# Keys loaded at a pace, reciprocals two steps later, and work moved between the blocks of the feed-forward, in a sandwich of attention and ternary feed-forward

## The chip, the core and the metric

The kernel runs on one core of a Trainium2 chip. The core has five engines that run side by side: TensorE (PE), which multiplies matrices; VectorE (DVE); ScalarE (ACT), which evaluates functions such as exp; GpSimd (POOL); and SyncE (SP), which here only issues transfers (DMAs). The engines meet through semaphores, and each works through its own instructions in order. The metric is the device time of one launch in microseconds (us), median of several runs.

## The reference

One input x of 4096 tokens by 256 features passes through attention and through a feed-forward. Each is given a normalized input and its output is normalized before it is added to the stream.

```python
def _layernorm(x, axis=-1, eps=1e-05):
    m = jnp.mean(x, axis=axis, keepdims=True)
    v = jnp.var(x, axis=axis, keepdims=True)
    return (x - m) / jnp.sqrt(v + eps)

# attention: H = 16 heads of 16, causal, float32
qkv = x @ w_attn + b_attn
logits = jnp.einsum('bhqd,bhkd->bhqk', q, k) * scale
logits = jnp.where(causal[None, None, :, :], logits, -jnp.inf)
weights = jax.nn.softmax(logits, axis=-1)
out = jnp.einsum('bhqk,bhkd->bhqd', weights, v)
return out.transpose(0, 2, 1, 3).reshape(b, n, d) @ w_proj + b_proj

# feed-forward: weights of -1, 0 and 1, tlin(x, w, s) = (x @ w.T) * s
h = jax.nn.silu(tlin(x, w1_w, w1_s)) * tlin(x, w2_w, w2_s)      # 256 -> 1024
h = jax.nn.gelu(tlin(h, h1_w, h1_s), approximate=False)         # 1024 -> 1024
h = jax.nn.gelu(tlin(h, h2_w, h2_s), approximate=False)         # 1024 -> 1024
return tlin(h, w3_w, w3_s)                                      # 1024 -> 256

x = x + _layernorm(attn(_layernorm(x)))
x = x + _layernorm(ffn(_layernorm(x)))
```

## The kernel before

**Blocks and items.** The tokens are cut into 8 blocks of 512 (`NB`, `QB`), a block into 4 tiles of 128 (`NT`). The first stage is the attention. An item (j, g) is block j of queries with 4 of the 16 heads; there are 32 items, numbered n = 4j + g. An item's inner loop (L855) runs over the 4(j+1) tiles of keys, kt.

**Three streams in an item.** Scores (`ScoreUnit`, tile `s`) of item n are made by PE and exponentiated by ACT (`e`, L661). Two steps later PE multiplies them with the values (`Values`, tile `av`); column 16 of each head's values is 1, so a row of `av` holds the sums of the exponentials. Meanwhile the row maxima of item n+1 are found: PE makes products (`pm`, L563) and DVE reduces them (`mx`, L576). All of it is issued in an order written out by hand, for PE in turns: products for maxima, scores, products for maxima, values. PE has three banks of memory for `pm`; if DVE stops, PE stops soon after.

**Keys.** A chunk is the keys of one block for one item: two loads of 256 KB from DRAM, where each number is held as a rounded half and the rest (`halves_of`). There are 16 places (`RING`). `ask(n, kt)` (L471), called at each step, asks for chunks of up to item n+2 as soon as the place's last user has been issued. All these loads go through SP's queue, as do the loads of queries and x and the stores of results. An instruction that waits on SP holds up what stands behind it.

**Background.** A `Background` holds a queue of generators, first in, first out. `pace` (L57) does as many steps of them per kt as their planned sizes ask for (`PREP`, `PROJECT`, `NORM` = 26, 28, 12). `prep(j)` makes queries, keys and values of a block, through the transposed input `xT` (tag `T`). `project(j)` (L212) is queued when the last `av` of block j has been stored to DRAM, that is in step 0 of block j+1: it loads x again and the sums of the exponentials (L221, tile `sums`), lets 3 steps pass, takes the reciprocals on DVE (L224), stores them, loads the attention's output (`o`) and the reciprocals spread over the heads (`inv`), multiplies them on POOL, projects on PE (`py`), normalizes and stores the stream as `x1[j]`. `norm_block(j)` (L290) loads `x1[j]`, normalizes it on DVE with a power on POOL (L172), and transposes it on PE (`ptf`); a function then takes the transposed features.

**Into the feed-forward.** In the last two items of attention `norm_block(0)` runs too; `first_features` (L771) lets ACT copy the result to `xT0` in float32. After the attention POOL issues loads of the scales (L892, L901), and a flag in memory decides between two branches; the profile took the first (`halves`), which holds for weights that survive the rounding. There the weights stay in memory, and each activation is a rounded half and the rest, on which PE multiplies one after the other. New pools of memory take over the places that the attention's pools held; the first use of such a pool waits for all users of what was there.

**A block of the feed-forward** (L1007): 8 output chunks with `za` = w1 and `zb` = w2 (L1011), Silu on ACT, a product `fa` on DVE (L1016) and the halving on DVE (`settle`, L965 and L966); then 8 chunks each of h1 and h2 (`z`, L1027) with Gelu and the halving; then 4 tiles of w3 (`pyf`, L1042), scaled, normalized, added to `x1` and stored (L1049 to L1058). Beside it runs a Background of its own, one step per output chunk: in block 0 first `project(7)`, queued ahead of the loop, then `norm_block(1)`, with two steps per chunk in h1 and h2; in the others `norm_block(j + 1)`.

Of the kernel before, what the change touches and what calls it, by code (L numbers as in the profile page):

```python
# [10 lines left out]
F32 = mybir.dt.float32  # L11
F32R = mybir.dt.float32r
AF = mybir.ActivationFunctionType
ALU = mybir.AluOpType
# [3 lines left out]
P = 128  # L18
QB = 512
NT = QB // P  # L20
# [47 lines left out]
def sandwich_kernel(  # L68
# [19 lines left out]
    nc = tc.nc  # L88
# [79 lines left out]
    def layernorm_rstd(mv):  # L168
        ve = stat.tile([P, NT], F32, tag="ve", name="ve")
        nc.vector.tensor_scalar_add(ve, mv[:, :, 1], EPS)  # L170
        rstd = stat.tile([P, NT], F32, tag="rstd", name="rstd")
        nc.gpsimd.tensor_tensor(rstd, ve, neghalf, ALU.pow)  # L172
        return rstd
# [38 lines left out]
    def project(j, room):  # L212
# [9 lines left out]
        for _ in range(3):  # L222
            yield True
# [96 lines left out]


    xT0 = const.tile([P, DC, QB], F32, tag="xT0", name="xT0")


    with ExitStack() as actx:
# [16 lines left out]
        class Room:  # L342
# [5 lines left out]
            def features(self, j):  # L348
                return [wk1.tile([P, DC, QB], F32, tag=t, name=f"{t}_{j}") for t in ("o", "inv")]
# [540 lines left out]
    def load_scale(pool, src, tag):  # L890
        s = pool.tile([P, FC], F32, tag=tag, name=tag)
        nc.gpsimd.dma_start(out=s, in_=src.rearrange("(c p) -> p c", p=P))  # L892
        return s

    fs = ctx.enter_context(tc.tile_pool(name="fs", bufs=1))
    s1 = load_scale(fs, w1_s, "s1")
    s2 = load_scale(fs, w2_s, "s2")
    sh1 = load_scale(fs, h1_s, "sh1")
    sh2 = load_scale(fs, h2_s, "sh2")
    s3 = fs.tile([P, D], F32, tag="s3", name="s3")  # L900
    nc.gpsimd.dma_start(out=s3, in_=w3_s.partition_broadcast(P))  # L901

    def feed_forward(halves):
# [6 lines left out]
        with ExitStack() as fctx:  # L910
# [23 lines left out]

            w3_r = fw.tile([P, FC, D], F32R, tag="w3", name=f"w3_{parts}")
            w3_sb = w3_r.bitcast(F32)
            if halves:
                tiles = {**W, "h2": weight_pieces("h2", TAGS["h2"])}
                load_pieces(rounded["h2"], tiles["h2"])
# [64 lines left out]
            room, bg = Room(), Background()  # L1004
            keep_features(0)([xT0[:, c, :] for c in range(DC)])
            bg.add("project", project(NB - 1, room), PROJECT)
            for j in range(NB):  # L1007
                xT = xTs[j]
                ha = activations(FC, f"ha{parts}_{j}")
                for oc in range(FC):  # L1010
# [9 lines left out]
                    bg.step()  # L1020
                if j + 1 < NB:
                    bg.add("norm", norm_block(j + 1, room, keep_features(j + 1)), NORM)
                src = ha
                for layer, (key, sc) in enumerate((("h1", sh1), ("h2", sh2))):
                    hb = activations(FC, f"hb{parts}_{j}_{layer}")
                    for oc in range(FC):
# [5 lines left out]
                        if j == 0:  # L1032
                            bg.step()
# [17 lines left out]
                rstd = layernorm_rstd(mv)  # L1051
                for t in range(NT):
                    normalize(y[:, t, :], y[:, t, :], mv, rstd, t)
                    nc.gpsimd.tensor_tensor(y[:, t, :], y[:, t, :], xb[j][:, t, :], ALU.add)  # L1054
                nc.sync.dma_start(
                    out=out[j * QB : (j + 1) * QB, :].rearrange("(t p) d -> p t d", p=P),
                    in_=y,
                )  # L1058
# [41 lines left out]
```

## Time and profile before

| | |
|---|---|
| median of 3 runs | 2531.14 us (2525.56 to 2536.95) |
| the profiled execution | 2537.64 us, its span 2535.9 us |
| mean granted clock of TensorE | 0.973 |
| busy: PE, DVE, ACT, POOL | 2415.0, 1787.8, 1310.2, 561.0 us |
| attention; feed-forward | to about 1813 us; from there on |
| DMA | 202.73 MB, mean 80 GB/s |

The span is that from the first to the last instruction; around it lie 1.7 us. A row of the profile names the engine, the line of the kernel, the operation and the tiles (out<-in). In brackets behind an instruction stands the idle time of its engine before it, and what ended it. `SPq` is SP issuing a transfer. Rows of a table of stretches give, behind the stretch, its length, the busy time (with the number of instructions) of PE, of PE's weight loads, of DVE, ACT and POOL, then PE's granted clock as a share of full speed, the share of the DMA engines that was busy, and GB/s.

### The profile page before, as it was taken

What the parts mean: (1) busy time and instruction counts of PE and PEld (TensorE: products, weight loads), DVE (VectorE), ACT (ScalarE), POOL (GpSimd) and SP (SyncE); (2) the same over time, 40 slices, a digit from 0 to 9 for tenths busy, and PEclk for the clock granted to TensorE, in tenths of its full rate; (3) what the DMA queues carried; (4) which work ended last, traced back from release to release, by engine and by line L of the source; (5) the groups of instructions that cost most, each with busy time, mean ns of one, the idle gap of its engine ahead of it and who ended that gap; (6) DMA issues with size and microseconds to landing.
All of it is one profiled execution on the core that took longest, in us unless ns stands there. A gap on an engine that the chain in (4) does not pass through costs nothing. (4 is left out here: it accounts for less than half of the span.)

```text
span 2535.9 us, 40119 instructions
## 1 busy us (share of the span) xinstructions
PE 2415.0 (95%) x15237; PEld 1437.1 (57%) x15237; DVE 1787.8 (70%) x3834; ACT 1310.2 (52%) x1712; POOL 561.0 (22%) x896
## 2 busy tenths in 40 slices
PE   5889999999999999999999999999899999999998
PEld 2545444545454454454555555544478787787776
DVE  1667887888897888797999989984145535554553
ACT  1336665666675667675766667767612222222221
POOL 2325332423243233322422231000120000000000
PEclk8779999999999999999999999999989999999999
DMA  4434434324233322423222232111310000000000
GB/s 154 158 127 153 133 115 161 96 98 130 98 126 126 101 71 72 158 92 130 92 77 66 88 100 73 51 43 51 100 34 17 17 1 17 17 17 1 17 9 10
DMA packets 134777, 202.73 MB, mean 80 GB/s; under 512 B 14864, under 2 KB 59536, under 8 KB 134576
## 3 DMA queue, kind: packets, MB, share of 16 engines
q1 hardware_dynamic: 132624, 198.75, 23.6%
q8 instruction: 122, 2.00, 0.3%
q10 hardware_dynamic: 1776, 1.18, 0.2%
q0 software_dynamic: 176, 0.15, 0.1%
q14 instruction: 79, 0.65, 0.1%
HBM read 137.91 MB, written 62.13 MB: 79 GB/s over the span
## 5 line engine op out<-in xcount | busy, mean ns | idle before, releaser
L661 ACT ACTIVATE e<-s 128x1024 f32<-128x1024 f32 (+3 forms) x1175 | 1038.7, 936 | 487.0 <-PE s L646 481.4
L576 DVE TENSOR_REDUCE mx<-pm 128x1 f32<-128x512 f32 x1792 | 1111.8, 682 | 161.0 <-PE pm L563 144.6
L563 PE MATMUL pm<-k,q 64*128 64x512 f32 (+3 forms) x2304 | 627.2, 455 | 44.8 <-DVE mx L576 33.0
L563 PEld LDWEIGHTS pm<-k,q 64*128 64x128 f32 x2304 | 324.1, 188 | 546.5 <-DVE mx L576 384.8
L696 PE MATMUL av<-e,v 128*32 128x512 f32 (+3 forms) x4608 | 584.4, 579 | 1.5 <-POOL e L666 1.5
L646 PE MATMUL s<-q,k 64*128 64x512 f32 (+3 forms) x2304 | 471.7, 391 | 4.4 <-ACT xT L515 1.3
L646 PE MATMUL s<-mrow,ones 64*128 64x512 f32 (+3 forms) x2304 | 458.1, 381 | 0.0
L1029 ACT ACTIVATE fb<-z,sh 128x512 f32<-128x512 f32 x128 | 88.1, 688 | 400.0 <-PE z L995 381.2
L580 DVE CUSTOM_DVE_ANT_0 pm<-pm,mask 128x384 f32<-128x384 f32 (+3 forms) x512 | 240.0, 517 | 76.5 <-PE pm L563 72.2
L646 PEld LDWEIGHTS s<-q,k 64*128 64x128 f32 x2304 | 235.8, 189 | 72.3 <-issue 18.4
L646 PEld LDWEIGHTS s<-mrow,ones 64*128 64x128 f32 x2304 | 240.7, 188 | 38.1 <-DVE mrow L620 0.7
L666 POOL TENSOR_SCALAR_AFFINE_SELECT e<-e 128x256 f32<-128x256 f32 x256 | 102.5, 407 | 637.4 <-ACT e L661 635.5
L995 PE MATMUL z<-hb_0h,h 128*128 128x512 f32 x512 | 203.8, 398 | 0.0
L995 PE MATMUL z<-hb_0l,h 128*128 128x512 f32 x512 | 203.0, 396 | 0.0
L696 PEld LDWEIGHTS av<-e,v 128*32 128x32 f32 x4608 | 91.8, 108 | 145.1 <-issue 129.9
L172 POOL TENSOR_TENSOR rstd<-ve,neghalf 128x4 f32<-128x4 f32 x19 | 19.3, 1015 | 687.3 <-DVE ve L170 661.6
L965 DVE CAST hb_1h<-fb 128x512 fp32r<-128x512 f32 x64 | 27.4, 428 | 150.7 <-ACT fb L1029 150.7
L965 DVE CAST hb_0h<-fb 128x512 fp32r<-128x512 f32 x64 | 28.3, 442 | 141.3 <-ACT fb L1029 141.3
L1014 ACT ACTIVATE sl<-za,s 128x512 f32<-128x512 f32 x64 | 44.1, 689 | 130.9 <-DVE fa L1016 65.7
L995 PEld LDWEIGHTS z<-hb_0l,h 128*128 128x128 f32 x512 | 97.1, 190 | 22.6
L995 PEld LDWEIGHTS z<-hb_0h,h 128*128 128x128 f32 x512 | 97.1, 190 | 22.6
L748 POOL CAST wh<-wc 128x256 fp32r<-128x256 f32 x88 | 34.9, 397 | 232.2 <-DMA wc<-in_h_t_dram 185.1
(247 smaller groups left out, 2463.9 us busy)
## 6 DMA issues: line engine op xcount, KB each, us to landing
k<-k SPq DMA_DIRECT2D x288, 256.0 KB
q<-q SPq DMA_DIRECT2D x64, 256.0 KB
x<-in_x_dram SPq DMA_DIRECT2D x16, 512.0 KB
k<-hik SPq DMA_DIRECT2D x32, 256.0 KB
k<-lok SPq DMA_DIRECT2D x32, 256.0 KB
q<-hiq SPq DMA_DIRECT2D x32, 256.0 KB
q<-loq SPq DMA_DIRECT2D x32, 256.0 KB
avd<-av_sb SPq DMA_DIRECT2D x32, 256.0 KB
```

The lines of the kernel that those rows point to most:

```text
L563: nc.tensor.matmul(ps[:, 0:n], lhsT=qT[j, g][pr][r, t * P : (t + 1) * P], rhs=kT[G * j + g, c, pr][r, 0:n], start=True, stop=True,)
L576: nc.vector.tensor_reduce(self.mx[:, h, c : c + 1], ps[:, 0:n], AX.X, ALU.max)
L580: nc.vector.tensor_tensor_reduce(out=ps[:, 0:n], in0=ps[:, 0:n], in1=mask[:, QB - n : QB], scale=1.0, scalar=-3.0e38, op0=ALU.add, op1=ALU ...
L646: nc.tensor.matmul(self.ps[i][:, self.q0 :], lhsT=(self.k, ones[pr])[m][r, :], rhs=(qT[j, g][pr], mT[j, g])[m][r, self.q0 :], start=(m == ...
L661: nc.scalar.activation(e[:, at : at + n, q0:], ps[:, :, q0:], AF.Exp)
L666: nc.gpsimd.affine_select(out=at, in_=at, compare_op=ALU.is_ge, fill=0.0, base=0, pattern=[[0, 2], [1, P]], channel_multiplier=-1,)
L696: nc.tensor.matmul(self.av[h * HW : (h + 1) * HW, q0:], lhsT=vb[kt // NT][:, kt % NT, o : o + HW], rhs=es[h // 2][:, h % 2, q0:], start=(k ...
L748: nc.gpsimd.tensor_copy(hi, w)
L965: nc.vector.tensor_copy(hi, full)
L995: nc.tensor.matmul(ps, lhsT=w[c], rhs=single(part[:, c, :]), start=(c == 0 and i == 0), stop=(c == kc - 1 and i == parts - 1),)
L1014: nc.scalar.activation(sl, za, AF.Silu, scale=s1[:, oc : oc + 1])
L1029: nc.scalar.activation(h, z, AF.Gelu, scale=sc[:, oc : oc + 1])
```

## The change

1. `ask`: from item 8 on (block 2), keys are asked for only at even kt, one chunk at a time.
2. `project`: 5 steps instead of 3 between the load of `sums` and its reciprocals, for blocks 2 to 6.
3. `first_features`: ACT writes the rounded half of `xT0`, DVE the rest; block 0 of the feed-forward reads these, without a conversion of its own.
4. The four loads of scales stand before the attention, in tiles of the constants' pool; `s3` is loaded inside the branch.
5. `project(7)` is queued in block 1 of the feed-forward, behind its w1 and w2, and the two steps per chunk are block 1's.
6. In the last block of the feed-forward each tile has its own power, normalization, sum and store, one tile behind the products; the sum of the last tile is DVE's.
7. Memory: `inv` shares the place of `xT` (tag `T`); the features of the feed-forward have one buffer (pool `f1`) instead of two.

```diff
     def layernorm_rstd(mv):
+        n = mv.shape[1]
...
-        nc.gpsimd.tensor_tensor(rstd, ve, neghalf, ALU.pow)
+        nc.gpsimd.tensor_tensor(rstd, ve, neghalf[:, 0:n], ALU.pow)
...
-        for _ in range(3):
+        for _ in range(5 if 1 < j < NB - 1 else 3):
             yield True
         nc.vector.reciprocal(sums, sums)
...
+    def load_scale(pool, src, tag):
+        s = pool.tile([P, FC], F32, tag=tag, name=tag)
+        nc.gpsimd.dma_start(out=s, in_=src.rearrange("(c p) -> p c", p=P))
+        return s
+
+    s1 = load_scale(const, w1_s, "s1")
+    s2 = load_scale(const, w2_s, "s2")
+    sh1 = load_scale(const, h1_s, "sh1")
+    sh2 = load_scale(const, h2_s, "sh2")
-    xT0 = const.tile([P, DC, QB], F32, tag="xT0", name="xT0")
+    xT0 = [
+        const.tile([P, DC, QB], F32R, tag=f"xT0{p}", name=f"xT0{p}") for p in "hl"
+    ]
...
-                return [wk1.tile([P, DC, QB], F32, tag=t, name=f"{t}_{j}") for t in ("o", "inv")]
+                return [wk1.tile([P, DC, QB], F32, tag=t, name=f"{t}o_{j}") for t in ("o", "T")]
...
                 if asked[0] >= RING and chunks[asked[0] - RING] >= (n, (kt - 1) // NT):
                     return
+                if n >= 2 * G and kt % 2:
+                    return
                 keys(*chunks[asked[0]])
+                if n >= 2 * G:
+                    return
...
-                nc.scalar.copy(xT0[:, c, :], pts[c])
+                hi, lo = (t[:, c, :] for t in xT0)
+                nc.scalar.copy(hi, pts[c])
+                nc.vector.tensor_tensor(lo, pts[c], hi, ALU.subtract)
...
+            s3 = fw.tile([P, D], F32, tag="s3", name=f"s3_{parts}")
+            nc.gpsimd.dma_start(out=s3, in_=w3_s.partition_broadcast(P))
...
-                    hp.tile([P, n, QB], F32, tag=f"h{n}{p}", name=f"{name}{p}")
+                    (f1 if halves and n == DC else hp).tile(
+                        [P, n, QB], F32, tag=f"h{n}{p}", name=f"{name}{p}"
+                    )
...
-            keep_features(0)([xT0[:, c, :] for c in range(DC)])
-            bg.add("project", project(NB - 1, room), PROJECT)
+            xTs[0] = [t.bitcast(F32) for t in xT0]
+            due = []
+
+            def leave(j, y, mv, ts, rstd):
+                for i, t in enumerate(range(ts.start, ts.stop)):
+                    nc.vector.tensor_scalar(
+                        y[:, t, :], y[:, t, :], mv[:, t, 0:1], rstd[:, i : i + 1],
+                        ALU.subtract, ALU.mult,
+                    )
+                    (nc.vector if (j, t) == (NB - 1, NT - 1) else nc.gpsimd).tensor_tensor(
+                        y[:, t, :], y[:, t, :], xb[j][:, t, :], ALU.add
+                    )
+                nc.sync.dma_start(
+                    out=out[j * QB + ts.start * P : j * QB + ts.stop * P, :].rearrange(
+                        "(t p) d -> p t d", p=P
+                    ),
+                    in_=y[:, ts, :],
+                )
...
+                if j == 1:
+                    bg.add("project", project(NB - 1, room), PROJECT)
...
-                        if j == 0:
+                        if j == 1:
                             bg.step()
...
+                    if j == NB - 1:
+                        one = slice(t, t + 1)
+                        due.append((j, y, mv, one, layernorm_rstd(mv[:, one, :])))
+                        while len(due) > (t < NT - 1):
+                            leave(*due.pop(0))
+                if j < NB - 1:
+                    leave(j, y, mv, slice(0, NT), layernorm_rstd(mv))
```

More of the change, by code (lines that the diff above doesn't have):

```diff
@@ L168, in layernorm_rstd @@
     def layernorm_rstd(mv):
-        ve = stat.tile([P, NT], F32, tag="ve", name="ve")
+        n = mv.shape[1]
+        ve = stat.tile([P, n], F32, tag=f"ve{n}", name="ve")
         nc.vector.tensor_scalar_add(ve, mv[:, :, 1], EPS)
-        rstd = stat.tile([P, NT], F32, tag="rstd", name="rstd")
-        nc.gpsimd.tensor_tensor(rstd, ve, neghalf, ALU.pow)
+        rstd = stat.tile([P, n], F32, tag=f"rstd{n}", name="rstd")
+        nc.gpsimd.tensor_tensor(rstd, ve, neghalf[:, 0:n], ALU.pow)
         return rstd
@@ L887, in sandwich_kernel @@
         bg.finish()
[L890 to L901, printed above, removed]
     def feed_forward(halves):
@@ L933, in tokens @@
                     return f1.tile([P, NT, D], F32, tag="y", name=f"yn_{j}_{parts}")
+            s3 = fw.tile([P, D], F32, tag="s3", name=f"s3_{parts}")
+            nc.gpsimd.dma_start(out=s3, in_=w3_s.partition_broadcast(P))
             w3_r = fw.tile([P, FC, D], F32R, tag="w3", name=f"w3_{parts}")
             w3_sb = w3_r.bitcast(F32)
+            room, bg = Room(), Background()
             if halves:
@@ L1002, in linear @@
                 return ps
-            room, bg = Room(), Background()
-            keep_features(0)([xT0[:, c, :] for c in range(DC)])
-            bg.add("project", project(NB - 1, room), PROJECT)
+            xTs[0] = [t.bitcast(F32) for t in xT0]
+            if not halves:
+                xTs[0] = activations(DC, "xTf0")
+                nc.vector.tensor_tensor(xTs[0][0], *xT0, ALU.add)
+            due = []
[14 more added lines that the diff above has]
+                )
             for j in range(NB):
@@ L1050, in feed_forward @@
                     layernorm_stats(y[:, t, :], mv, t)
[L1051 to L1058, printed above, removed]
+                    if j == NB - 1:
[5 more added lines that the diff above has]
+                    leave(j, y, mv, slice(0, NT), layernorm_rstd(mv))
     low = nc.values_load(flag, min_val=0, max_val=1)
```

## The prediction

> **What bounds the kernel now.** I read the page first: TensorE (PE) is busy 2415.0 of 2535.9 us, so what can be won is in the 121 us where it is not, and in the time when its clock is halved.
>
> ```profile
> span 2535.9 us, 40119 instructions
> PE 2415.0 (95%) x15237; PEld 1437.1 (57%) x15237; DVE 1787.8 (70%) x3834; ACT 1310.2 (52%) x1712; POOL 561.0 (22%) x896
> ```
>
> The view of waits then shows who could be late for PE at a place that the change touches: `sums` makes VectorE (DVE) wait seven times (us in total, times, longest), and SP's issue of that load waits for the store of `avd` to land.
>
> ```profile
> DVE sums L224 <- DMA sums<-avd: 23.9, 7, 7.0
> ...
> SPq L221 <- DMA avd<-av_sb: 24.0, 7, 4.8
> ```
>
> The times of those waits, from the instructions in order of time, give the places. A table of 20 us stretches from the beginnings of blocks 2 to 7 gives the price: busy PE in the third column, its clock in the column of 1.00s.
>
> ```profile
> 272.00:292.00 20.00, 17.11 (x113) 7.82 (x110) 13.53 (x35) 11.04 (x12) 2.97 (x4) 0.83 0.56 174
> 434.00:454.00 20.00, 16.66 (x106) 7.92 (x104) 12.67 (x28) 10.03 (x11) 4.66 (x6) 0.83 0.49 165
> 636.00:656.00 20.00, 17.52 (x132) 9.13 (x132) 15.79 (x33) 12.13 (x14) 7.64 (x10) 1.00 0.52 176
> 878.00:898.00 20.00, 18.38 (x128) 9.05 (x124) 15.51 (x32) 12.08 (x13) 8.00 (x10) 0.91 0.61 185
> 1163.00:1183.00 20.00, 16.15 (x100) 7.16 (x99) 11.60 (x26) 9.53 (x10) 5.93 (x8) 0.83 0.63 208
> 1478.00:1498.00 20.00, 20.00 (x152) 10.70 (x151) 18.13 (x38) 15.13 (x17) 4.04 (x6) 1.00 0.54 164
> ```
>
> Idle PE is 2.9, 3.3, 2.5, 1.6, 3.9 and 0 us; lost clock, (1 - clock) x 20, is 3.4, 3.4, 0, 1.8, 3.4 and 0. In between PE is full (296.3 of 300 us from 1200 to 1500), so neither is made good later. Block 7 shows what an undisturbed start looks like, and SP's order of issue says why:
>
> ```profile
> 868.84 3.82 SPq L443 DMA_DIRECT2D k<-k  x8
> 873.37 0.32 SPq L707 DMA_DIRECT2D avd<-av_sb  x1
> 879.15 0.58 SPq L221 DMA_DIRECT2D sums<-avd  x1
> ...
> 1479.27 0.32 SPq L707 DMA_DIRECT2D avd<-av_sb  x1
> 1481.52 0.55 SPq L221 DMA_DIRECT2D sums<-avd  x1
> ```
>
> With eight key loads (2 MB) ahead of it, the store of `avd` lands 5.8 us after issue; with none, 2.25 us.
>
> **Part 1: keys paced, reciprocals later.** At the start of an item 6, 8, 10, 8 and 4 key loads (blocks 2 to 6) become 2. The store should land some 2.2 to 3 us after issue, not 4.9 to 5.8; `sums` then lands 2.2 us later (277.04 to 279.27), 2 to 3 us earlier than now. The two added yields move the reciprocal by one step of the key loop in block 3 (the pace there, 52 / 46, gives two background steps each) and by two in blocks 4 to 7 (52 / 58 and less give one), at 2.7 us a step (1479.78, 1482.48 and 1485.18 for the `av` products). Waits of 3.2, 3.5, 2.7, 1.8 and 4.4 us lose 2 to 8 us each: only block 2, which gets the pacing alone, may keep some 0.3 us. Gain: idle 2.9 + 3.3 + 2.5 + 1.6 + 3.9 = 14.2, clock 3.4 + 3.4 + 0 + 1.8 + 3.4 = 12.0, together 26.2, less 0.3 = **25.9**.
>
> Here a rule weighs against me. The Trainium skill (TensorE: Matmul & The Clock Gate, section "What's actually happening") lets the clock fall after an idle window of about 3.4 us. By it only block 6's gap of 3.9 us costs clock, and part 1 would give 14.2 + 3.4 - 0.3 = 17.3. The rows show halved clock after gaps of 1.6, 2.9 and 3.3 us, none after 2.5. I take the rows; the difference of 8.6 goes into the range.
>
> What else moves: `project` yields 29 times against a planned size of 28, so its store of `x1` falls out of the pace; in block 6, with no `prep` behind it, it waits for block 7. Its reader is far off in the feed-forward: nothing. `inv` now shares `T` with `xT`; both belong to one first-in-first-out background, each done before the other begins: nothing, and without that cover one `inv` landing, about 4.9 us of POOL's wait, off PE's path. Later keys: block 7 loads chunk c of item n+2 at step 4c+6 instead of 4c+5. Its last chunk still comes at step 0 of item n+1 and is first needed about step 4: 10 us of slack.
>
> **Part 2: from attention to feed-forward.**
>
> ```profile
> 1811.42 1.14 POOL L892 DMA_DIRECT2D s<-in_w_s_dram  x1 [0.20 <-issue]
> 1813.06 0.41 PE L696 MATMUL av<-e,v 128*32 128x128 f32 x4 [1.38 <-POOL e L666]
> 1816.86 1.14 ACT L980 CAST xTf_0h<-xT 128x512 fp32r<-128x512 f32 x2 [2.76 <-DMA avd<-av_sb]
> 1821.72 0.75 DVE L1016 SCALAR_TENSOR_TENSOR fa<-zb,s,sl 128x512 f32<-128x512 f32 x1 [2.92 <-issue]
> 1836.62 0.55 DVE L224 RECIPROCAL sums<-sums 128x64 f32<-128x64 f32 x1 [7.00 <-DMA sums<-avd]
> 1845.49 0.51 PE L995 MATMUL z<-ha_0l,h 128*128 128x512 f32 x1 [1.18 <-DVE ha_0l L966]
> ```
>
> Four things in a row go: the scale load that POOL runs ahead of the last mask (1.38 us of PE), the conversion, which waits for the last store's landing, the wait for `s2` (DVE stands until 1821.72), and the reciprocal's 7.0 us, behind which four `fa` are queued. New path: last `av` 1813.06 - 1.38 = 1811.68, end 1812.1; copy of `av` 0.6, and `za` starts near 1812.8, as its inputs stand in tiles that attention never gave up. Silu needs its table (1.28) and `za`: 1814.2 to 1814.9. DVE takes eight rounds of 1.86 (1823.94 to 1825.81): 1814.9 + 14.9 = 1829.8, where now it is 1845.4. Gain 15.6, and the halved window that I read behind it (8 products of 0.63 from 1846.4) 1.7: **17.3**. If Silu's tile too waits for the store (landing 1815.4, then table 1.28 and Silu 0.7), DVE starts at 1817.4 and the gain is 14.8: the low end. PE's eight rounds of 1.87 stay under DVE's.
>
> Moved to block 1: SP's loads of x, `sums`, o and inv twice each and stores of `invd` and `x1`; POOL's two products and norm; 16 `py` products of 3.5 us. They cost there what they cost here, and SP issues them behind the store of block 0's result, no longer behind 16 loads of h2. The load of `s3` (0.56 us of POOL) is wanted only by block 0's last products, 70 us on: nothing. `sums` can land during w1 and w2, at least 15 us before its reciprocal in h1: no wait. The double steps keep one flaw: norm and transposes are background steps 27 and 28. Now they share one output chunk in block 0, and PE stands 3.74 us at 1884.5; with 2k+1 and 2k+2 as a chunk's steps they share chunk 13 in block 1. Zero gain. The single-buffered features are written only after the block's w1 and w2 products: nothing.
>
> **Part 3: the end.** Now: `ve` 2525.47, power 1.02, four normalizations, four sums on POOL (to 2530.23), store at 2530.26, landed 2533.45. After: the same to 2526.78, one normalization 0.55 and one sum on DVE 0.42, store at about 2527.9 behind that of tile 2. Gain 2.4, and some 1.0 because 128 KB land sooner than 512 KB (not shown; 0 to 1.5, the time in which 512 KB passed): **3.4**. The extra DVE work per earlier tile (0.17 + 0.55) fits the 1.9 us that PE needs for a tile.
>
> **Part 4: costs.** Four scale loads stand at the start, 3.8 us of POOL (1.14, 0.91, 2 x 0.88), which is not wanted before 14.28. Their packets are another matter: from 2 to 9 us the DMA engines are full (share 1.02), and the products wait for `wp` until 9.35. In the trace one load is 16 packets of about 0.35 us, one an engine: 4 x 0.35 = 1.4 at worst, 0 if they fall behind `wp`; I take **1.2**. First features: DVE gets two subtractions (0.69 each) that wait for ACT's casts, with the maxima, and so PE's `pm`, behind them, and both score buffers stay held: 0 to 1.6, I take **0.8**.
>
> **Sum.** 25.9 + 17.3 + 3.4 - 1.2 - 0.8 = 44.6. The profiled execution took 2537.6 (span and 1.7 around it): 2493.0. It lies 6.5 over the median of the runs, 2531.1; if the same waits were in those, 2486.5. Some of the 6.5 may be waits that go anyway: I take **2490**.
>
> **Rivals.** (a) Attention recovers only idle time, or half its waits stay because `sums` is late for another reason: -9 to -15, about 2502. For it: the rule above; against it, block 7. (b) Small waits of PE for DVE fall too, as bursts of keys thin out: up to 10 more, 2480. (c) Most gains go to new waits in the same places (DVE behind `sums` again, feed-forward bound by the store): 2525. Against it: all the named waits have a shown releaser that moves. (d) Slower: keys late. In blocks 5 to 7 the ring is the limit; if loads landed over 10 us later than now, PE would stop in each item. It takes 12.7 + 41 = 54 us over 12 items, 4.5 us each, thus keys about 15 us late, to end at 2544. Only one wait of PE for a key load, 2.4 us near 80, stands in the profile.
>
> **How the numbers follow.** Likeliest 0.72 (2482 to 2499), (a) 0.12, (b) 0.08, (c) 0.05, (d) 0.03. The range from 2478 to 2506 leaves out (c), (d) and the far parts of (a) and (b). Within 0.5% (12.7 us, about what a measurement tells from no change) is most of (c): faster 0.93, same 0.04, slower 0.03.
>
> **What would show it.** Right: `sums` holds DVE under 1 us in blocks 2 to 7; the clock is 1.00 in the rows above; `za` begins within 1 us of the last `av`; the reciprocal of block 7 waits for nothing; a gap near 3.7 us before the transposes in block 1; start later by about 1 us. Wrong: PE waiting for `k`, `za` waiting for the store, or as many halved windows as now.

## The result, and the profile after

The kernel after takes 2493.03 us (median of 6 runs, 2490.62 to 2495.86), the kernel before beside it 2534.47 us: a ratio of 0.984 (95% interval 0.9825 to 0.9858), or 41 us. The forecast was 2490 with a range from 2478 to 2506. The profiled execution took 2495.86 us. Its page begins:

```profile
span 2494.2 us, 40139 instructions
PE 2395.7 (96%) x15237; PEld 1434.2 (58%) x15237; DVE 1786.7 (72%) x3838; ACT 1309.1 (52%) x1710; POOL 561.6 (23%) x898
```

The same 15237 products keep PE busy 19.3 us less than before, although no product was taken out. Part of that is clock; the rest, as will be seen, is that one kind of product became faster.

The view of waits (us in total, times, longest) answers the two rows on `sums`: VectorE waits 2.8 us instead of 23.9.

```profile
DVE sums L225 <- DMA sums<-avd: 2.8, 2, 2.6
```

Of these 2.8, block 1 has 2.6, where neither half of part 1 is at work, and block 2 has 0.26 (0.17 to 1.72 in the other eight traces of kernels with both halves). These are the 20 us stretches at the beginnings of blocks 2 to 7, with the columns as before (third column PE busy, the column of 1.00s its clock):

```profile
276.00:296.00 20.00, 20.00 (x136) 10.26 (x133) 17.34 (x45) 12.22 (x13) 6.50 (x7) 1.00 0.49 154
434.00:454.00 20.00, 19.60 (x137) 10.11 (x135) 17.17 (x40) 12.22 (x13) 6.40 (x7) 1.00 0.52 162
636.00:656.00 20.00, 20.00 (x156) 10.50 (x156) 18.46 (x42) 14.40 (x15) 6.17 (x8) 1.00 0.43 132
873.00:893.00 20.00, 20.00 (x153) 10.23 (x154) 18.47 (x37) 14.57 (x16) 6.12 (x8) 1.00 0.51 156
1155.00:1175.00 20.00, 20.00 (x154) 10.29 (x154) 18.45 (x37) 14.49 (x15) 7.99 (x10) 1.00 0.67 206
1475.00:1495.00 20.00, 20.00 (x156) 10.37 (x155) 18.35 (x37) 14.26 (x15) 5.81 (x7) 1.00 0.44 134
```

PE is full and at full clock in all but 0.4 us. SP's order of issue at block 5 shows why: two key loads stand ahead of the store, not eight, and the load of the sums, which waits for the store, follows 2.3 us later instead of 5.8.

```profile
858.54 0.90 SPq L456 DMA_DIRECT2D k<-k  x2
863.06 0.32 SPq L725 DMA_DIRECT2D avd<-av_sb  x1
863.43 0.43 SPq L113 DMA_DIRECT2D x<-in_x_dram  x1
865.36 0.59 SPq L222 DMA_DIRECT2D sums<-avd  x1
```

From attention to feed-forward (instructions in order of time; in brackets the idle time before one, and what ended it). First the row of before, then those of after:

```profile
1817.53 0.79 PE L995 MATMUL za<-xTf_0h,w 128*128 128x512 f32 x1 [4.06 <-ACT xTf_0h L980]
```

```profile
1797.36 0.58 ACT L723 COPY av_sb<-av 128x512 f32<-128x512 f32 x1 [1.13 <-PE av L714]
1798.00 0.50 PE L1007 MATMUL za<-xT0h,w 128*128 128x512 f32 x1 [0.69 <-ACT av_sb L723]
...
1799.27 1.28 ACT L1046 ACT_TABLE_LOAD   x1 [1.33 <-PE za L1007]
...
1801.29 0.75 DVE L1048 SCALAR_TENSOR_TENSOR fa<-zb,s,sl 128x512 f32<-128x512 f32 x1 [72.24 <-ACT sl L1046]
```

`za` starts 0.69 us after the last `av`, where it stood 4.06 us before, and VectorE starts 0.7 us after Silu's table is there. Silu's tile did not wait for the store: what ACT stands for, 1.33 us ahead of its table, is `za`. The table follows `za` instead of running beside it, and VectorE starts 4.0 us after the end of the last `av`, some 1.2 us later than the forecast had it.

What got worse is at the start; the gap ahead of the transposes has moved to block 1. First the two rows of before, then those of after:

```profile
9.35 2.05 PE L811 MATMUL pb<-wp,bv 128*128 128x256 f32 x4 [9.35 <-DMA wp<-in_w_proj_dram]
...
1888.21 2.21 PE L307 MATMUL ptf<-ident,yn 128*128 128x128 f32 x8 [3.74 <-DVE yn L176]
```

```profile
3.75 1.76 POOL L324 DMA_DIRECT2D sh<-in_h_s_dram  x2
...
12.10 2.05 PE L831 MATMUL pb<-wp,bv 128*128 128x256 f32 x4 [12.10 <-DMA wp<-in_w_proj_dram]
...
1956.11 2.21 PE L308 MATMUL ptf<-ident,yn 128*128 128x128 f32 x8 [3.74 <-DVE yn L177]
```

The first product starts at 12.10 instead of 9.35; the gap of 3.74 us ahead of the transposes stands in block 1 now.

By stages of the two profiled executions (us; the ends of a stage are starts of PE's products or of the copy of the last `av`; the last product counts to its end):

| stage | before | after | gain | forecast |
|---|---|---|---|---|
| to the first product | 9.35 | 12.10 | -2.75 | -1.2 |
| first product to copy of the last `av` | 1804.2 | 1785.3 | 18.9 | 25.9 - 0.8 |
| from there to block 2 of the feed-forward | 195.0 | 177.7 | 17.3 | 17.3 |
| block 2 to the last product | 515.8 | 510.9 | 4.9 | 0 |
| last product to the end | 11.6 | 8.2 | 3.4 | 3.4 |
| sum | 2535.9 | 2494.2 | 41.8 | 44.6 |

The sum is near, but it hides two errors of opposite sign: attention gave 6 us less than forecast in this pair of profiles, and blocks that the forecast held unchanged became faster. The experiments begin with the second.

### The profile page after: what moved, and what is told of

It is laid out like the page before. It is cut to its first block, busy times and chain, and to the rows that moved or that the text cites. A ratio compares the mean times of both kernels' runs of the same rounds, so it can differ in the third digit from the quotient of the medians.

```text
span 2494.2 us, 40139 instructions
## 1 busy us (share of the span) xinstructions
PE 2395.7 (96%) x15237; PEld 1434.2 (58%) x15237; DVE 1786.7 (72%) x3838; ACT 1309.1 (52%) x1710; POOL 561.6 (23%) x898
## 4 chain that ended last, share of the span: by engine, by line
PE 82%; DVE 11%; issue 2%; DMA 2%; ACT 1%; POOL 1%; SPq 0%; ACTq 0%; POOLq 0%; DVEq 0%
PE av L714 20%; PE s L664 18%; PE z L1007 18%; PE pm L581 16%; DVE mx L594 3%; DVE pm L598 2%; PE pyf L1076 2%; DVE fa L1048 2%; PE pk L426 1%; PE py L249 1%; PE pv L543 1%; PE pq L426 1%; PE pmt L630 1%; PE za L1007 1%; PE zb L1007 1%
## 5 line engine op out<-in xcount | busy, mean ns | idle before, releaser
L173 POOL TENSOR_TENSOR rstd<-ve,neghalf 128x4 f32<-128x4 f32 (+1 forms) x22 | 20.7, 943 | 662.9 <-DVE ve L171 637.4
L977 DVE CAST hb_0h<-fb 128x512 fp32r<-128x512 f32 x64 | 27.3, 427 | 138.7 <-ACT fb L1063 138.7
L1048 DVE SCALAR_TENSOR_TENSOR fa<-zb,s,sl 128x512 f32<-128x512 f32 x64 | 47.6, 745 | 72.2 <-ACT sl L1046 72.2
```

The costliest lines, as they stand in the source:

```text
L977: nc.vector.tensor_copy(hi, full)
L1048: nc.vector.scalar_tensor_tensor(h, zb, s2[:, oc : oc + 1], sl, ALU.mult, ALU.mult)
```

## The experiments

Times beside a run are medians. Each is set against the kernel before, run beside it on the same chip (2532 to 2534 us in the three sets of runs), and against the kernel after (2493.0; once more in the last set: 2491.7).

### 1 and 2. Why feed-forward blocks became faster

A block of the steady feed-forward takes 86.15 us before and 84.90 after, with the same products. From the starts of the products in the trace, those of `z` follow each other at a median of 232 ns before and 227 after (their pitch), while `py` (216), `pyf` (120) and a full item of the attention (75.4 us) are unchanged. What differs is the place of the tiles in memory (addresses are those of the built kernels; a trace does not hold them). The change moved sizes about, and the feed-forward's own tiles, the activations among them, start 128 bytes past a multiple of 256 before and at a multiple of 256 after; the weights of `za`, `zb` and `z` start at multiples of 256 in both. In these products the activations are the moving operand (`rhs`) and the weights the stationary one (`lhsT`). Two kernels shift the feed-forward's tiles and leave these weights where they are.

The kernel after, shifted:

```diff
+            pad = fw.tile([P, 32], F32, tag="pad", name=f"pad_{parts}")
+            nc.vector.memset(pad, 0.0)
             s3 = fw.tile([P, D], F32, tag="s3", name=f"s3_{parts}")
```

> The kernel after, with 128 bytes of unused space ahead of the feed-forward's tiles: its activations (the moving operands of za, zb, z) then start at 128 past a multiple of 256 bytes, as they did in the kernel before, and the weights stay where they are. Theory A, the start address of the moving operand sets the pace of the products: the start-to-start pitch of the z products goes from 227 back to 232 ns, a steady feed-forward block from 84.9 to 86.1 us, and the whole to about 2503 us (2500 to 2506), 10 us over the kernel after; the attention stays the same. Rival B, the blocks got faster through what moved out of block 0 or through the loads that no longer lie beside them: pitch 227, block 84.9, total within 2 us of the kernel after (2493).

The kernel before, aligned:

```diff
-        s = pool.tile([P, FC], F32, tag=tag, name=tag)
+        i = ("s1", "s2", "sh1", "sh2").index(tag) * FC
+        s = scales[:, i : i + FC]
...
+    scales = const.tile([P, D], F32, tag="junk", name="scales")
     s1 = load_scale(fs, w1_s, "s1")
```

> The kernel before, with its four scale tiles put into a dead tile of the attention, so that everything behind them lies 128 bytes lower and the activations of the feed-forward start at multiples of 256 bytes; nothing else differs. Theory A (start address of the moving operand): pitch of the z products 227 instead of 232 ns, steady block 84.9 instead of 86.1 us, total about 10 us under the kernel before (2521 to 2527 where that takes 2534). Rival B (what moved in the change made the blocks faster): pitch 232, total within 2 us of the kernel before.

The shifted one took 2503.4 us (2492.1 to 2504.5; ratio to before 0.988, 0.9864 to 0.990), the aligned one 2522.1 (2515.0 to 2531.9; 0.996, 0.9950 to 0.9972). The group of the largest `z` products in the kernels before, before aligned, after, and after shifted (busy us, mean ns of one product):

```profile
L995 PE MATMUL z<-hb_0h,h 128*128 128x512 f32 x512 | 203.8, 398 | 0.0
```

```profile
L997 PE MATMUL z<-hb_0h,h 128*128 128x512 f32 x512 | 201.0, 393 | 0.0
```

```profile
L1007 PE MATMUL z<-hb_0h,h 128*128 128x512 f32 x512 | 200.8, 392 | 0.0
```

```profile
L1009 PE MATMUL z<-hb_0h,h 128*128 128x512 f32 x512 | 204.3, 399 | 0.0
```

In these four kernels a product is 5 to 7 ns shorter where the moving operand starts at a multiple of 256. The pitch is 232, 227, 227 and 232 ns, the steady block 86.15, 84.9, 84.9 and 86.2 us. Theory A holds against its rival in both directions: the change is worth some 10 us here that it didn't set out to win. That it is the activations, and no other tile that was shifted with them, block 0 of the kernel after shows: there only the features lie elsewhere, 32 past a multiple, and `za` and `zb` have 233 to 234 ns, `z` 227. What about their address counts is the next question.

### 3. How fine the alignment is

```diff
+            if halves:
+                nc.vector.memset(fw.tile([P, 16], F32, tag="pad", name="pad64"), 0.0)
             s3 = fw.tile([P, D], F32, tag="s3", name=f"s3_{parts}")
...
                 y = f1.tile([P, NT, D], F32, tag="yf", name=f"yf{parts}_{j}")
+                if halves and j == 0:
+                    nc.gpsimd.memset(f1.tile([P, 8], F32, tag="pad", name="pad32"), 0.0)
```

> The kernel after with the feed-forward's transposed inputs (moving operand of za and zb) moved to 64 past a multiple of 256 bytes, and its hidden layers (moving operand of z) to 96 past one. Theory A, only multiples of 256 bytes give the short pitch: za, zb and z all at 231 to 234 ns. Theory B, multiples of 64 bytes are enough: za and zb 227 from block 1 on, z 232. The earlier kernels had only 32, 128 and 160 past a multiple beside 0. Time about 2503 (2498 to 2507) in A, about 2501 in B; the pitch decides, not the time.

It took 2502.8 us in its one run. `z` at 96 past a multiple has the long pitch, 232. `za` and `zb` at 64 past one have 229.5 (block 1) and 229 (block 2), between the two. Neither theory is right: here 64 costs half of what 32, 96, 128 or 160 past a multiple cost. The tiles at 32 past one are block 0's features in the kernel after, those at 160 the same tiles in the kernel of experiment 8 (235).

A trace taken for another question says that the moving operand's own address is not what counts. The kernel of experiment 10 has some small tiles fewer, and all that lies behind them, the weights too, starts 64 past a multiple of 256. Its `z` products have 227 ns, and so have `za` and `zb` from block 1 on:

```profile
L1007 PE MATMUL z<-hb_0h,h 128*128 128x512 f32 x512 | 200.3, 391 | 0.0
```

What fits all 14 traces is how far apart a product's two operands start, modulo 256 bytes: 227 ns at 0, 229 to 230 at 64, 231 to 237 at 32, 96, 128, 160 and 224 (block 0 of experiment 10, features at 32 against weights at 64: 232 to 233). `pyf` agrees where both its operands moved together, from 128 past to 0: it kept 120 ns. But with 32 between them, in the kernel of this experiment, it had 117, so in these products of 256 columns the distance costs nothing. No kernel here moved the weights alone, and why the distance counts is open.

### 4. The same for attention's scores

The queries, exponentials, values and score offsets of the attention start 96 bytes past a multiple of 256.

```diff
-        bv = aw.tile([P, DC], F32, tag="bv", name="bv")
+        first = wk1.tile([P, NT, D], F32, tag="y", name="first")
+        bv = first[:, 0, 0:DC]
...
-        bqk = aw.tile([P, 2 * DC], F32, tag="bqk", name="bqk")
+        bqk = biases
...
-        two = aw.tile([P, 2], F32, tag="two", name="two")
+        two = first[:, 1, 0:2]
...
-    neghalf = const.tile([P, NT], F32, tag="neghalf", name="neghalf")
+    small = const.tile([P, NT + 2 * DC], F32, tag="small", name="small")
+    neghalf, biases = small[:, 0:NT], small[:, NT:]
```

> The kernel after with 96 bytes of small tiles of the attention put elsewhere, so that the tiles behind them (values, score offsets, queries, exponentials) start at multiples of 256 bytes instead of 96 past one. Theory A, what held for the feed-forward's moving operands holds for the scores' too: a pair of score products takes 227 to 228 instead of 231 to 234 ns from start to start, 2304 pairs save 8 to 12 us, a full attention item is 1 to 1.5% shorter, and the total is -10 us (-6 to -18) against the kernel after. Rival B: with half-height operands the start address does not matter, or another engine paces the items: pairs as before, total within 2 us.

A miss: 2493.5 us (2491.6 to 2495.2), and the group of score products is as it was, 407 ns in the kernel after (first row) and here (second).

```profile
L664 PE MATMUL s<-q,k 64*128 64x512 f32 x1920 | 411.9, 407 | 2.0 <-ACT xT L533 1.2 <-ACT e L679 0.5
```

```profile
L666 PE MATMUL s<-q,k 64*128 64x512 f32 x1920 | 412.6, 407 | 2.0 <-ACT xT L535 1.2 <-ACT e L681 0.5
```

The commonest times for a pair of score products are 231 and 236 ns, not 227. These products run two at a time on half the rows; their keys start at multiples of 256, so the distance of the operands went from 96 to 0 here, and why it costs nothing stays open. Full height is not the condition either: the products of `pq`, 128 rows by 512 columns in plain float32, had theirs go from 96 to 0 too and take 607 ns in both kernels. The finding is shown for the feed-forward's `za`, `zb` and `z`, on rounded halves, and no further.

### 5 to 7. Pacing, delay, and both: what part 1 is made of

The kernel after with the delay undone:

```diff
-        for _ in range(5 if 1 < j < NB - 1 else 3):
+        for _ in range(3):
             yield True
```

> The kernel after with three steps instead of five between the load of the sums and the reciprocal, the pacing of the keys kept. Theory A, both halves of the first part are needed: the sums land some 4 us after the last item's store, the reciprocal reaches VectorE about 2 us too early in blocks 2 to 5 and 7 of the order (projections 1 to 6), waits 1 to 3 us each, and TensorE runs dry at those places; the waits of VectorE on the sums come to 6 to 12 us over the five projections, total +5 us (2 to 9) over the kernel after. Rival B, the pacing alone brought the gain and the delay is slack: waits under 1 us each, total within 1.5 us.

The kernel after with the pacing undone:

```diff
-                if n >= 2 * G and kt % 2:
-                    return
                 keys(*chunks[asked[0]])
-                if n >= 2 * G:
-                    return
```

> The kernel after with the keys asked for as in the kernel before (all that fit, at every step) and the five steps kept. Theory A, the pacing is what lets the store and the sums through: the store of the item's values lands 4.9 to 5.8 us after its issue instead of 2.2 at the starts of the blocks, VectorE waits 1 to 4 us on the sums in block 2 and shorter in later ones, total +9 us (5 to 15) over the kernel after. Rival B, the delay alone brought the gain: the store is late again but VectorE's wait on the sums stays under 0.5 us in every block, total within 2 us.

The kernel before with the pacing alone:

```diff
+                if n >= 2 * G and kt % 2:
+                    return
                 keys(*chunks[asked[0]])
+                if n >= 2 * G:
+                    return
```

> The kernel before with the pacing of the keys alone (from block 2 on at every second step, one chunk at a time); three steps before every reciprocal, as before. Theory A, the pacing by itself brings the first part's gain, the two further steps add nothing: the store of the values lands about 2.2 us after its issue at the starts of blocks 2 to 5, VectorE's waits on the sums of projections 1 to 6 fall from 15.6 us to under 4, and the total is 20 us (16 to 26) under the kernel before. Rival B, the two measures stand in for each other only in part, and each alone brings half: total 10 to 14 us under.

VectorE's waits on the sums at the starts of blocks 2 to 6, in us, with the time from the issue of the store to that of the load of the sums:

| kernel | time | 2 | 3 | 4 | 5 | 6 | store to load |
|---|---|---|---|---|---|---|---|
| before | 2534 | 3.21 | 3.52 | 2.67 | 1.80 | 4.43 | 4.9 to 5.8 |
| pacing alone | 2515.1 | 1.10 | 0 | 0 | 0 | 2.76 | 2.2; block 6: 5.7 |
| after without pacing | 2499.6 | 3.31 | 1.24 | 0 | 0 | 0 | 5.2 to 6.1 |
| after without delay | 2494.1 | 0.41 | 0 | 0 | 0 | 3.25 | 2.1 to 2.3; block 6: 6.0 |
| after | 2493.0 | 0.26 | 0 | 0 | 0 | 0 | 2.2 to 2.3; block 6: 5.9 |

Each half covers most of what the other covers. The pacing is what makes the store quick, and alone it brings 19 us (ratio 0.9926, 0.9902 to 0.9950), near the 20 of theory A. It leaves 1.10 us in block 2, where the delay isn't at work, and 2.76 in block 6, where 8 loads of w1 and w2 stand in the queue and the store is late whatever the keys do. There, and only there, the delay is needed. The row at block 6's beginning with the pacing alone has what its absence costs, 2.2 us of idle PE and 3.4 of clock:

```profile
1141.00:1161.00 20.00, 17.81 (x110) 8.24 (x110) 14.41 (x24) 10.66 (x12) 8.00 (x10) 0.83 0.57 175
```

The kernel after without the delay has this wait too, 3.25 us, and still no time to show for it (2491.5 to 2500.6; ratio to before 0.986, 0.9841 to 0.9875): by the median rival B is right, by the trace theory A in one of five places, and the difference is smaller than the spread of the runs. Without the pacing the store is late again everywhere, and the delay hides that in blocks 4 to 6, in part in block 3 and not at all in block 2, where it isn't at work:

```profile
277.00:297.00 20.00, 17.01 (x110) 8.02 (x103) 13.40 (x30) 10.65 (x12) 5.25 (x6) 0.83 0.39 127
437.00:457.00 20.00, 18.89 (x138) 9.79 (x130) 16.16 (x39) 12.35 (x13) 5.26 (x6) 1.00 0.44 140
637.00:657.00 20.00, 20.00 (x153) 10.10 (x154) 18.35 (x37) 14.81 (x16) 6.72 (x10) 1.00 0.40 132
```

It costs 6.5 us (ratio to before 0.988, 0.9869 to 0.9898), in the range of theory A (5 to 15).

### 8. The two costs of the change, taken out

```diff
-    s1 = load_scale(const, w1_s, "s1")
-    s2 = load_scale(const, w2_s, "s2")
-    sh1 = load_scale(const, h1_s, "sh1")
-    sh2 = load_scale(const, h2_s, "sh2")
...
+            if (j, g) == (3, 1):
+                s1, s2, sh1, sh2 = (
+                    load_scale(const, *pair)
+                    for pair in ((w1_s, "s1"), (w2_s, "s2"), (h1_s, "sh1"), (h2_s, "sh2"))
+                )
...
-                        if j == 1:
+                        if j == 1 and (layer, oc) != (0, 0):
                             bg.step()
```

> The kernel after with two edits far apart in time: the four scale loads are issued in block 3 of the attention instead of at the start, and the first double step in the feed-forward's block 1 is a single one, so that the normalisation and the transposes of the next block's tile stand on both sides of a chunk of products. Theory A: the first product starts at 9.4 us instead of 12.1 (the small scattered loads were what made the load of wp late), TensorE's gap of 3.7 us ahead of ptf falls to under 1 and the half clock behind it goes: together -8 us (-5 to -10) against the kernel after. Rival B: wp is late for another reason (first product still at 12), or the transposes then wait just as long for POOL's rstd (gap still over 2 us): the one or the other part stays, -3 to -5.

2482.6 us (2478.5 to 2485.9; ratio to before 0.979, 0.9758 to 0.9818), 10 under the kernel after. Both rows are as theory A has them:

```profile
9.41 2.05 PE L827 MATMUL pb<-wp,bv 128*128 128x256 f32 x4 [9.41 <-DMA wp<-in_w_proj_dram]
...
1951.80 1.64 PE L308 MATMUL ptf<-ident,yn 128*128 128x128 f32 x8 [0.80 <-DVE yn L177]
```

The four small loads had cost 2.7 us. The 3.74 us ahead of the transposes were the two background steps sharing a chunk, as the forecast read it: one step omitted sets a chunk of products between them, and the gap is 0.80.

### 9. Block 7's projection back in block 0

```diff
+            bg.add("project", project(NB - 1, room), PROJECT)
             due = []
...
-                if j == 1:
-                    bg.add("project", project(NB - 1, room), PROJECT)
...
-                        if j == 1:
+                        if j == 0:
                             bg.step()
```

> The kernel after with block 7's projection and its double steps put back into the feed-forward's block 0. Theory A, the move is what removes the stall after the attention: the load of the sums waits behind the weights' transfers for the last store (12 to 15 us from store to load in the kernels with it in block 0), VectorE waits 4 to 7 us on the sums, TensorE runs dry, the double steps' gap of 3.7 us goes back from block 1 to block 0, and the total is +8 us (5 to 13) over the kernel after. Rival B, without the scale loads and with the first features as halves there is enough slack in block 0: the wait on the sums is under 2 us and the total within 2 us of the kernel after.

2504.9 us (2503.0 to 2506.1; ratio to before 0.988, 0.9851 to 0.9906), 12 over the kernel after. The reciprocal waits as it did before, and PE behind it:

```profile
1808.70 1.24 SPq L222 DMA_DIRECT2D sums<-avd  x1
1816.31 0.55 DVE L225 RECIPROCAL sums<-sums 128x64 f32<-128x64 f32 x1 [7.72 <-DMA sums<-avd]
...
1817.49 0.80 PE L1007 MATMUL z<-ha_0h,h 128*128 128x512 f32 x1 [6.03 <-DVE fa L1049]
```

The load of the sums is issued 12.5 us after the store, against 14.8 in the kernel before: what else the change did there leaves the store almost as late. Theory A.

### 10. The last norm over all tiles at once

```diff
-                    if j == NB - 1:
+                    if j == NB:
...
-                if j < NB - 1:
+                if j < NB:
                     leave(j, y, mv, slice(0, NT), layernorm_rstd(mv))
```

> The kernel after with the last block's norm over all four tiles at once again and one store, instead of tile by tile. Theory A: from TensorE's last product to the end of the span 11.6 us as in the kernel before, instead of 8.3. Rival B: the tail is set by the last store's landing alone and stays within 1 us of 8.3. Total +3 us of 2493; a single time can't tell that, the tail in the trace does.

From the end of the last product to the end of the span: 11.4 us (2474.9 to 2486.3) instead of 8.2. Theory A; the single time, 2488.0, says nothing, as expected.

### 11. The kernel after once more: where the half clock falls

> The kernel after once more, as the measure for the runs beside it. If the half-clock windows lie on a grid of 3.41 us whose phase differs from run to run, as the eight traces so far have it, then the places of the windows behind gaps of 0.6 to 1.9 us differ from the first profile of this kernel, while the gaps themselves stay within 0.1 us: some that had a window have none, and the other way round. If a window is tied to its place in the program, the same places have them again (362, 1415, 1456, 1664, 1954, 1995, 2251 us). Total 2493 (2489 to 2499).

2491.7 us (2486.7 to 2495.1). From 300 us on the gaps are those of the first profile to within 0.05 us; the windows are not. Of those at 364, 1415, 1456 and 2251 none came again; those behind the gaps near 1655, 1719, 1949 and 1990 did; a new one stands at 2333, behind a gap of 0.62 that had none. Up to the last product, the windows of the 14 traces of this case all begin on a grid of 3.413 us (none is off it by more than 0.004), last whole steps of it, and the grid's phase against the start differs from run to run. So a gap's cost depends on how a run's grid cuts it. Two neighbouring steps of the first profile of the kernel after, twice, each with the same gap of 0.62 us and the smaller one behind it:

```profile
1991.96:1995.37 3.41, 2.16 (x7) 0.79 (x6) 3.06 (x6) 0.39 (x1) 0.00 (x0) 1.00 0.00 0
1995.37:1998.78 3.41, 3.41 (x9) 2.65 (x10) 1.12 (x2) 0.69 (x1) 0.00 (x0) 0.50 0.02 5
2162.63:2166.04 3.41, 2.32 (x9) 1.14 (x7) 3.27 (x7) 1.16 (x1) 0.00 (x0) 1.00 0.00 0
2166.04:2169.45 3.41, 3.19 (x13) 2.42 (x14) 1.67 (x3) 0.69 (x1) 0.00 (x0) 1.00 0.02 5
```

A step with 1.25 us of idle PE is followed by one at half clock, one with 1.09 is not. I counted the steps at full clock of the 14 traces, from 180 us on, by the idle PE in them. In the feed-forward behind block 0's start, none of 2527 with up to 1.05 us is followed by half clock, 4 of 34 between 1.05 and 1.12, and 31 of 36 above. In the attention it takes more: 11 of 6447 below 1.2 us, 12 of 21 between 1.2 and 1.6, and all 28 above 1.6. Eight of the 11 stand at one place of the program, between 1444 and 1453 us, each in another trace and with only 0.25 to 0.40 us of idle PE, so idle time isn't all that counts; what else does is open. In the feed-forward a step needn't be idle throughout: a third of it was enough.

### 12. A version that beats both

Each feed-forward block but the first loses 0.62 us ahead of `z` and 0.4 within it, because VectorE begins the block with the last block's norm. This kernel has the edits of experiment 8, and gives that norm's subtraction and scaling to GpSimd:

```diff
-                    nc.vector.tensor_scalar(
+                    (nc.vector if j == NB - 1 else nc.gpsimd).tensor_scalar(
                         y[:, t, :], y[:, t, :], mv[:, t, 0:1], rstd[:, i : i + 1],
```

> The kernel with the scale loads in block 3 and the first double step single, and besides the last norm's subtraction and scaling of blocks 0 to 6 on GpSimd instead of VectorE. Theory A: in the feed-forward VectorE begins every block with 2.2 us of that work and a wait of 1.2 us for the reciprocal root, starts the chain of fa late, never catches up at 1.86 us a round against TensorE's 1.81, and so TensorE waits 0.62 us ahead of z<-ha_h and about 0.4 after it in each of blocks 1 to 7; with it gone these 7 x 1.05 = 7.4 us and one or two half-clock windows go: 2473 us (2469 to 2477), 9 under the kernel with the two edits alone (2482.6). Rival B: the rounds of 1.86 us by themselves leave VectorE late, the gaps fall by half at most: 2477 to 2482.

2467.7 us (2465.1 to 2471.6; ratio to before 0.9749, 0.9736 to 0.9762): 15 less than experiment 8 and more than theory A gave it. The idle time ahead of `z` is gone (in the kernel after this group waits 0.9 us):

```profile
L1008 PE MATMUL z<-ha_3h,h 128*128 128x512 f32 x64 | 24.9, 390 | 0.0
```

A block takes 82.83 us instead of 84.9, all from block 2 on within 0.1 us, and the feed-forward has no half-clock window before the last product. That is 2.07 us a block, not the 1.05 of theory A. The groups of `z` on `ha_3` have 1.4 of it as idle time in the kernel after (0.9 and 0.5); the rest stands in no row as idle.

## Why the prediction was right, and where it was wrong

**Part 1, at its places: right.** From the last item of a block to the first of the next, the gain is 5.4, 5.1, 3.4, 3.4 and 7.0 us for blocks 2 to 6, together 24.4 of the 25.9. The clock's share was real. With 17.3, the sum by the rule of the Trainium skill (TensorE: Matmul & The Clock Gate, section "What's actually happening"), seven of these would be missing. That page's free-running window of 3413 ns is what the traces show; its condition, an idle window, is not: in the feed-forward a window with a third of idle time was enough (experiment 11). The grid also fits the one gap that had puzzled the forecast, 2.5 us without half clock: it was cut into 1.04 and 1.44, and between 1.2 and 1.6 the attention's steps went either way.

**Part 1, for the attention as a whole: too high, by how much is open.** In this pair of profiles attention gained 18.9 instead of 25.1. The idle time came as forecast: from 180 us on, PE's waits for VectorE in the attention sum to 34.6 us before and 21.2 after, 13.4 of the 14.2. What is missing is clock, outside the block starts: there the profile after has 27.3 us at half clock from 300 us on, all but one of 3.4 behind gaps of 0.65 to 1.9 us that before has too, where before has 10.2 at such places; half of the difference, 8.5 us, is lost time. The step that failed is to take the half-clock windows of one profile as fixed, those at the block starts as a cost to remove and those elsewhere as unchanged ("in between PE is full, so neither is made good later"). Nothing was made good, but windows at unchanged gaps came and went: in the second trace with the attention of before, that of experiment 2, the starts of blocks 2 to 6 lost 8.5 us of clock and not 12.0. The attention of after took 1776.7 to 1785.3 us in the six traces that have it, and that of before 1804.2 and 1795.3 in its two. The gain is thus 10 to 27 us by the pair one takes, and 20 between the middles. By medians the pacing alone gives 19.

Of the signs of being wrong none came: from 180 us to the last product the time at half clock fell from 54.6 to 41.0 us in this pair, and to 20.5 in the second trace of the kernel after.

**Part 2: right, with a different make-up.** The total is 17.3 as forecast, but about 2.5 of it are the shorter pitch in blocks 0 and 1 (2 x 1.25), so the mechanism itself gave about 15; the table that follows `za` is 1.2 of what is missing. Experiment 9 shows its core, the wait on the sums, to be worth 12. The double steps' gap moved to block 1 at its old size, 3.74, with a half-clock window behind it in both: zero gain, as said.

**What was not forecast: the address.** "They cost there what they cost here" and the silence on blocks 2 to 7 assumed that a product's pace is given by its shape. The list of the change had the memory item in it, and I read it for lifetimes only. Experiments 1 and 2 put some 10 us on the place of the activations by medians; in the profile blocks 2 to 7 show only 4.9, since two half-clock windows fell there.

**Part 3: right**, 3.4, of which experiment 10 shows 3.2.

**Part 4: one term too small, one too large.** The scale loads cost 2.75, twice the upper end of 1.4. That end came from their packets' own time, 4 x 0.35; but between 6 and 11 us the 1 KB packets of the queue of `wp` took 94 ns on average beside them (76 in the second trace of the kernel after), and 51 to 52 without (before, experiment 8), so they slowed others' packets, not only displaced them. The first features' subtractions cost nothing that shows: the gap near 1660 is 1.91 us, with or without them, and comes with VectorE's wait of 1.1 us for the norm's root.

**The choice of 2490** moved the sum of 2493.0 towards the median; the result is at the unmoved sum, but that is luck: attention's shortfall and the address nearly cancelled. Of the rivals, (a) came near in its first half, as attention did give less, and the experiments refute its reason; (b) brought nothing: PE's waits for VectorE under 0.6 us in the attention, from 180 us on, sum to 13.9 us before and 13.7 after; (c) and (d) found no place: no wait of PE for a key after 85 us in the trace of after.

## What to carry to other kernels

When a change moves tiles in memory, compare where both operands of a product start before you call an untouched stage unchanged: here 128 bytes were worth 10 us. Half-clock windows behind short gaps are drawn anew in each run, so count a gap by its chance of filling a third of a 3.41 us step (the bound in this feed-forward), not by what one profile shows, and shorten gaps below that. Take several traces before you explain a few us of a long stage: the same attention differed by 9 us here. Two remedies for one wait are not worth their sum; try each alone.

## What the runs showed of the hardware

- A feed-forward product of 128 rows by 512 columns on rounded halves follows the last one after 227 ns if its moving and its stationary operand start equally far past a multiple of 256 bytes (both at 0, or both at 64), after 229 to 230 with 64 bytes between them, and 231 to 237 with 32, 96, 128, 160 or 224. Pairs of products on half the rows, plain float32 products (`pq`) and products of 256 columns (`pyf`) lost nothing by a distance (96, 96 and 32 bytes).
- TensorE's clock is set in steps of 3.413 us on a grid whose phase is free. A step with over 1.1 us (feed-forward) or 1.6 us (attention) of idle time was followed by one at half clock in 31 of 36 and 28 of 28 cases. Why the bound is higher in the attention, and why one place there fell with 0.25 to 0.40 us, is open.
- Four loads of 4-byte pieces, 16 KB in all, issued by GpSimd at the start made a 256 KB load on another queue land 2.7 us later: the first product starts at 11.9 to 12.3 us in the nine traces with them and at 9.4 to 9.5 in the five without.
